# A decoder layer on one core: cross exponentials and the fourth slot's normalisations in other places of ACT's order

## The chip, the cores and the metric

The kernel runs on one core of a Trainium2 chip. The core has a matrix engine (TensorE, PE in the profile, its weight loads PEld), a vector engine (VectorE, DVE), an activation engine (ScalarE, ACT), a general engine (GpSimd, POOL), and SyncE (SP), which issues nearly all transfers here. Each engine takes its own instructions one after another, and semaphores hold an instruction back until what it needs is there. The metric is the device time of one execution in microseconds (us); less is better.

## The reference

One layer of a decoder, in float32, for 32 sequences of 256 tokens with 256 features:

```
x = layernorm(x + self_attention(x))           # 16 query heads, 4 key heads of 64; rotary; alibi bias
x = layernorm(x + cross_attention(x, ctx))     # 16 heads of 16; windows of 64; mask by cell numbers
x = layernorm(x + ffn(x))                      # 256 -> 1024 (gate, up) -> 256, ternary weights, 8 bit rows
```

Self-attention has a softmax over all 256 keys. Cross-attention normalises its query, its context and its output before their projections, rotates queries and keys, and lets a token see the causal part of its own window and the window before it, where the cell numbers agree. The feed-forward rounds its activations by the largest absolute value of a row, and its gate is silu.

## The kernel before

**Periods and slots.** The program is one loop over *slots* (from line 891); four slots, `part` 0 to 3, make a *period* `m`. A sequence has eight self-attention units (128 queries, four heads each), two per period: `2 * m` and `2 * m + 1`. It has four cross-attention units (128 queries, eight heads each), one per period, `k = m - 4`: a sequence's cross-attention runs in the four periods after its self-attention, beside the next sequence's self-attention. So a sequence takes four periods, called P0 to P3 below. Everything else (projections, output projections, normalisations, the feed-forward) is written as generators that yield the number of slots until their next piece; `parts()` runs the pieces that are due in a slot.

**What a unit does.** Self: `self_scores` (L392 on TensorE, name s; then four L408 on DVE, which add the alibi bias and give the negative row maximum nm), `self_exp` (two L426 on ACT per half of the unit; a unit has halves 0 and 1), `self_turn` (eight transposes L453, name t, and two copies L458 on ACT, name pT), `self_values` (L470, name o, and ACT's copy L477, name oT), `self_spread` and `self_normal` (L485, name R; DVE's L493). Cross: `cross_scores` (L662, name xs, and eight L676 on DVE, giving xnm), `cross_exp` (four L692 on ACT per half, name xp), `cross_turn` (L701, name xt, and ACT's copy L703, name xpT), `cross_values` (L717, name xo, and ACT's copy L726, name xoT), `cross_back` (L737, name xr).

**Deferred closures.** Some pieces put a closure on the list `last`, and `flush()` runs the list at the end of the slot (in the kernel before: of every slot). The closures are: in `self_output`, `residual`, with zq (DVE L526) and x1 (ACT L527, then POOL L528); the scalings by ACT of line 197 (`scaled`): the context tokens cs in `cross_inputs`, the cross output on, the two results x of later layernorms; and the store of out. The closures of a fourth slot are, from a period to the next:

- P0 to P1: residual of the sequence's predecessor's second token block (zq, x1);
- P1 to P2: two scalings of cs, which wait for POOL's rstd_zc;
- P2 to P3: the scaling y (L197, the second block's final layernorm of a sequence three places before), its store to out, and residual of the first token block (zq, x1);
- P3 to P0: none.

zq is then transposed on TensorE (name zqT, L203), copied by ACT (zT, L204) and multiplied (xq, L538); ACT adds the bias (L556, name qb). This happens in P1 for one token block and in P3 for the other. In P3, too, fall the gate matmuls of the feed-forward (L804, name ff) and their tanh on ACT (L818), then DVE's L819.

**What sets the order.** For TensorE, DVE and ACT the order is the order in which the program is written (`manual_schedule`, line 888); POOL's and SP's instructions are put in order by the compiler's scheduler. All PSUM tiles come from one pool of eight banks, so an early release by ACT or DVE lets a later matmul begin. The feed-forward's input goes through two transposing transfers on SP (L797, name xiT), and the rotary halves through four transfers (L311, name other, from psin).

Of the kernel before, what the change touches and what calls it, by code (L numbers as in the profile page):

```python
# [50 lines left out]
def kernel(  # L51
# [139 lines left out]
    def flush():  # L191
        while last:
            last.pop(0)()
# [694 lines left out]
    with tc.manual_schedule(engines={mybir.EngineType.PE, mybir.EngineType.DVE, mybir.EngineType.Activation}):  # L888
        running = []
        slot = min(starts)  # L890
        while starts or running:
            m, part = divmod(slot, 4)
            k = m - CROSS
            for gen in starts.pop(slot, ()):
                running.append([slot, gen])

            def cross(f, unit, *more):
                if 0 <= unit < 4 * B:
                    f(*divmod(unit, 4), *more)

            def pair(f, unit):
                if 0 <= unit < 4 * B:
                    f(*divmod(unit, 4))

            def own(f, unit, *more):
                if 0 <= unit < 8 * B:
                    f(*divmod(unit, 8), *more)

            def parts():
                for r in list(running):  # L910
                    if r[0] == slot:
                        wait = next(r[1], r)
                        if wait is r:
                            running.remove(r)
                        else:
                            r[0] += wait or 1

            if part == 0:
                own(self_scores, 2 * m)
                own(self_scores, 2 * m + 1)  # L920
                own(self_exp, 2 * m, 0)
                own(self_exp, 2 * m, 1)
                own(self_exp, 2 * m + 1, 0)
                pair(self_values, m - 1)
                pair(self_spread, m - 1)
                cross(cross_turn, k - 1, 0)
                cross(cross_turn, k - 1, 1)
                own(self_exp, 2 * m + 1, 1)
                parts()
                pair(self_normal, m - 1)  # L930
            elif part == 1:
                parts()
                cross(cross_scores, k)
                cross(cross_values, k - 1)
                cross(cross_exp, k, 0)
            elif part == 2:
                parts()
                cross(cross_exp, k, 1)
                own(self_turn, 2 * m)
                cross(cross_back, k - 1)  # L940
            else:
                pair(self_inverse, m)
                own(self_turn, 2 * m + 1)
                parts()
            flush()
            slot += 1

# [86 lines left out]
```

## Time and profile before

| what | value |
|---|---|
| median of 3 runs | 2207.41 us (2206.43 to 2208.82) |
| the profiled execution's own time | 2208.47 us |
| its span | 2206.7 us |
| granted TensorE clock, mean | 0.984 |
| busy: PE, DVE, ACT, POOL | 96%, 79%, 75%, 50% |
| busy PE from 200 to 2060 us | 1846.04 of 1860 us |

The profile is of one execution. Its span runs from the first to the last instruction of the program; the execution's time lies 1.8 us above it. A group of instructions has its line, engine, operation and `written<-read` names, and how often it came; a wait is named by who waited for whom. The end of a matmul is modelled, so the starts are what to go by. Times in the text are positions in this span unless a unit of difference is meant.

### The profile page before, as it was taken

To read this page: it belongs to the slowest core of one execution; us is meant where nothing else is said; L and a number is where in the kernel's file an instruction comes from. 1 tells how busy PE (TensorE), PEld (TensorE's weight loads), DVE (VectorE), ACT (ScalarE), POOL (GpSimd) and SP (SyncE) were. 2 spreads that over 40 slices of the span, in tenths; PEclk is the share of its full clock that TensorE was granted. 3 is DMA by queue.
4 is the path that set the end of the run, shared out by engine and by line. 5 is a ranking of instruction groups with operands and counts; after the bars stand their busy time and mean duration, and the time that the engine had idled before them with its cause. 6 is when DMAs were issued, how large, how long until landed. Compare 5 with 4: busy or idle time off the path is not lost.

```text
span 2206.7 us, 55094 instructions
## 1 busy us (share of the span) xinstructions
PE 2127.6 (96%) x17766; PEld 1658.8 (75%) x17828; DVE 1742.3 (79%) x6949; ACT 1660.3 (75%) x4961; POOL 1107.7 (50%) x1849
## 2 busy tenths in 40 slices
PE   7899999999999999999999999999999999999984
PEld 5687777777777777777777777777777777777752
DVE  3676888878888878888888888888788887888775
ACT  2578778787778877778877778777778887777862
POOL 4454554555554545554545554545555545555442
PEclk9999999999999999999999999999999999999996
DMA  6322222222222223222222222222222222222111
GB/s 208 94 59 56 68 58 61 60 61 71 70 60 59 64 56 72 70 61 59 64 57 73 68 60 61 61 61 69 71 64 58 61 61 64 71 63 54 31 42 31
DMA packets 191424, 144.05 MB, mean 65 GB/s; under 512 B 107808, under 2 KB 160928, under 8 KB 191136
## 3 DMA queue, kind: packets, MB, share of 16 engines
q1 hardware_dynamic: 189440, 136.95, 25.0%
q8 instruction: 142, 2.33, 0.4%
q10 hardware_dynamic: 1696, 3.57, 0.4%
q14 instruction: 146, 1.20, 0.2%
HBM read 39.50 MB, written 8.39 MB: 22 GB/s over the span
## 4 chain that ended last, share of the span: by engine, by line
PE 77%; ACT 8%; DVE 8%; DMA 2%; issue 2%; POOL 1%; SPq 0%; ACTq 0%; POOLq 0%; DVEq 0%
PE wo L501 10%; PE proj L329 10%; PE t L453 10%; PE s L392 8%; PE o L470 8%; ACT p L426 5%; PE ff L804 4%; PE xt L701 4%; PE xq L538 3%; PE xs L662 3%; PE ffo L851 3%; PE xk L610 3%; PE xv L622 2%; PE R L485 2%; PE xw L763 2%; PE v L361 2%
## 5 line engine op out<-in xcount | busy, mean ns | idle before, releaser
L426 ACT ACTIVATE p<-p,nm 128x256 f32<-128x256 f32 x1024 | 508.3, 499 | 241.8 <-DVE nm L408 241.8
L408 DVE CUSTOM_DVE_ANT_0 p<-s,alibi 128x256 f32<-128x256 f32 x1024 | 361.6, 416 | 3.2 <-PE s L392 3.2
L692 ACT ACTIVATE xp<-xp,xnm 128x128 f32<-128x128 f32 x1024 | 328.5, 401 | 33.8 <-DVE xnm L676 33.8
L458 ACT COPY pT<-t 128x512 f32<-128x512 f32 x512 | 263.9, 598 | 9.4 <-PE t L453 9.2
L453 PE MATMUL t<-ident,p 128*128 128x128 f32 x2048 | 266.0, 273 | 0.9 <-ACT p L426 0.9
L392 PE MATMUL s<-kT,qT 64*128 64x256 f32 x2048 | 259.1, 391 | 0.0
L676 DVE CUSTOM_DVE_ANT_0 xp<-xs,mask 128x128 f32<-128x128 f32 x1024 | 225.7, 286 | 37.2 <-PE xs L662 37.2
L353 POOL TENSOR_TENSOR qT<-qT,other 128x512 f32<-128x512 f32 x128 | 163.2, 1275 | 182.8 <-DMA other<-psin 100.5
L470 PE MATMUL o<-pT,v 128*64 128x256 f32 x2048 | 250.3, 386 | 0.4 <-ACT pT L458 0.4
L329 PE MATMUL proj<-xT,wq_sb 128*128 128x256 f32 x1024 | 245.8, 384 | 0.0
L501 PE MATMUL wo<-wo_sb,oT 128*128 128x256 f32 x1024 | 244.6, 382 | 0.0
L453 PEld LDWEIGHTS t<-ident,p 128*128 128x128 f32 x2048 | 233.7, 141 | 9.2 <-ACT p L426 2.7
L392 PEld LDWEIGHTS s<-kT,qT 64*128 64x128 f32 x2048 | 191.8, 186 | 62.3 <-POOL mask L603 11.9
L501 PEld LDWEIGHTS wo<-wo_sb,oT 128*128 128x128 f32 x1024 | 193.5, 192 | 28.6 <-DVE gu L297 0.3
L470 PEld LDWEIGHTS o<-pT,v 128*64 128x64 f32 x2048 | 136.0, 136 | 99.2 <-issue 31.1
L329 PEld LDWEIGHTS proj<-xT,wq_sb 128*128 128x128 f32 x1024 | 187.7, 193 | 21.6
L426 ACT ACTIVATION_READ_ACCUMULATOR p<-p,nm 128x1 f32 x1024 | 194.0, 189 | 0.0
L493 DVE TENSOR_TENSOR oT<-oT,R 128x512 f32<-128x512 f32 x128 | 87.9, 687 | 104.5 <-ACT oT L477 102.8
L840 POOL TENSOR_SCALAR gu<-gu,ffhup 128x1024 f32<-128x1024 f32 x64 | 72.0, 1125 | 184.5 <-DVE ffhup L836 184.5
L819 DVE SCALAR_TENSOR_TENSOR gu<-gu,ff 128x512 f32<-128x512 f32 x128 | 82.3, 684 | 96.4 <-ACT gu L818 96.4
L600 POOL TENSOR_SCALAR mask<-ck_i,cq_sb 64x128 f32<-64x128 f32 (+1 forms) x96 | 70.3, 732 | 142.7 <-DVE xnm L676 136.7
L703 ACT COPY xpT<-xt 128x512 f32<-128x512 f32 x256 | 135.5, 579 | 0.8 <-PE xt L701 0.7
(148 smaller groups left out, 4480.4 us busy)
## 6 DMA issues: line engine op xcount, KB each, us to landing
other<-psin SPq DMA_DIRECT2D x640, 64.0 KB, 2.0
xT<-in_xt_dram SPq DMA_DIRECT2D x32, 256.0 KB, 2.7
xs<-in_x_dram SPq DMA_DIRECT2D x32, 256.0 KB, 2.7
cs<-in_ctx_dram SPq DMA_DIRECT2D x32, 256.0 KB, 2.8
other<-qb SPq DMA_DIRECT2D x64, 128.0 KB, 2.0
kTz<-tr SPq DMA_DIRECT2D x256, 32.0 KB, 2.0
other<-qb SPq DMA_DIRECT2D x128, 64.0 KB, 1.9
out_dram<-x SPq DMA_DIRECT2D x32, 256.0 KB, 2.1
```

The costliest lines, as they stand in the source:

```text
L329: nc.tensor.matmul(pq[:, c * L : (c + 1) * L], w[:, dc, c * P : (c + 1) * P], xT[:, dc, :], start=(dc == 0), stop=(dc == NDC - 1),)
L353: nc.gpsimd.tensor_tensor(d2, d2, other, ALU.add)
L392: nc.tensor.matmul(banks[half][:, rr * L : (rr + 1) * L], qT[rows_, rr, qc * P : (qc + 1) * P], kT[rows_, kc, :], start=(rr == 0), stop=(r ...
L408: nc.vector.tensor_tensor_reduce(p[:, cols], banks[half][:, cols], alibi[:, 2 * (4 * kc + 2 * rp + rr) + half, :], -0.125, 3.0e38, ALU.add ...
L426: nc.scalar.activation(p[:, cols], p[:, cols], AF.Exp, bias=nm[:, rr : rr + 1], scale=-1.0, accum_out=s["sums", i // 2][:, e : e + 1],)
L453: nc.tensor.transpose(pt[:, j * P : (j + 1) * P], p[half][:, rr * L + kk * P : rr * L + (kk + 1) * P], ident,)
L458: nc.scalar.copy(pT[half], pt)
L470: nc.tensor.matmul(po[half * HD : (half + 1) * HD, rp * L : (rp + 1) * L], s["v"][:, kk, (2 * kc + half) * HD : (2 * kc + half + 1) * HD], ...
L501: nc.tensor.matmul(py[:, 0:D], s["oT", qc, kc][:, r, :], wo_sb[:, 4 * kc + r, :], start=(kc == 0 and r == 0), stop=(kc == 1 and r == 3),)
L676: nc.vector.tensor_tensor_reduce(p[:, cols], banks[2 * half + j // 2][:, j % 2 * P : (j % 2 + 1) * P], s["mask"][:, qc, :], -1.0, 3.0e38, ...
L692: nc.scalar.activation(p[:, cols], p[:, cols], AF.Exp, bias=s["xnm", i][half][:, j : j + 1], scale=-1.0)
L703: nc.scalar.copy(pT, pt)
```

## The change

Three things are put elsewhere in the written order; no instruction is added or removed.

- In the first slot, unit `2 * m`'s exponentials are written straight behind its scores, then the closures of the fourth slot before are run, and then come unit `2 * m + 1`'s scores.
- The fourth slot no longer flushes at its end. Behind the loop a last flush is added for what is left.
- The cross exponentials of half 0 go from the end of the second slot to the third, behind `self_turn(2 * m)`; those of half 1 go from the third slot, ahead of `self_turn(2 * m)`, to the end of the fourth, behind `self_turn(2 * m + 1)` and `parts()`.

```diff
             if part == 0:
                 own(self_scores, 2 * m)
-                own(self_scores, 2 * m + 1)
                 own(self_exp, 2 * m, 0)
                 own(self_exp, 2 * m, 1)
+                flush()
+                own(self_scores, 2 * m + 1)
                 own(self_exp, 2 * m + 1, 0)
                 pair(self_values, m - 1)
                 pair(self_spread, m - 1)
...
                 parts()
                 cross(cross_scores, k)
                 cross(cross_values, k - 1)
-                cross(cross_exp, k, 0)
             elif part == 2:
                 parts()
-                cross(cross_exp, k, 1)
                 own(self_turn, 2 * m)
+                cross(cross_exp, k, 0)
                 cross(cross_back, k - 1)
             else:
                 pair(self_inverse, m)
                 own(self_turn, 2 * m + 1)
                 parts()
-            flush()
+                cross(cross_exp, k, 1)
+            if part < 3:
+                flush()
             slot += 1
+        flush()
```

## The prediction

> **What bounds the kernel now.** I read the page's busy table, then busy time by stage, then the waits, then the order of time at each place where the change moves something.
>
> The page, parts 1 and 2:
>
> ```profile
> PE 2127.6 (96%) x17766; PEld 1658.8 (75%) x17828; DVE 1742.3 (79%) x6949; ACT 1660.3 (75%) x4961; POOL 1107.7 (50%) x1849
> ...
> PE   7899999999999999999999999999999999999984
> ```
>
> Busy time by stage (us; PE, weight loads, DVE, ACT, POOL):
>
> ```profile
> 200.00:2060.00 1860.00, 1846.04 (x15684) 1447.21 (x15738) 1519.46 (x6108) 1464.99 (x4391) 966.11 (x1609) 1.00 0.26 63
> ```
>
> Of these 1860 us TensorE is idle for 14. The waits name nearly all of it (total, times, longest):
>
> ```profile
> ACT p L426 <- DVE nm L408: 241.8, 95, 22.8
> ACT cs L197 <- POOL rstd_zc L185: 87.7, 33, 8.3
> PE xq L538 <- ACT zT L204: 13.5, 32, 0.9
> ```
>
> TensorE runs its written order with one regular pause of about 0.36 us per sequence, before xq; outside it only the first 100 us and the last 150 have idle TensorE time. ACT's long waits cost nothing by themselves. The diff leaves TensorE's order as it is: self_exp, cross_exp and the deferred closures issue nothing there. So the question is where ACT or DVE, in their new order, come late for TensorE.
>
> I call the four periods of a sequence (65.67 us together) P0 to P3; one lies at 1197.83 (P0), 1212.55 (P1), 1227.71 (P2), 1249.66 (P3), 1263.50 (next P0), the times of their first self scores. The pause is in P3. ACT there:
>
> ```profile
> 1247.24 0.63 ACT L197 ACTIVATE x<-x,rstd_y 128x256 f32<-128x256 f32 x1
> 1247.74 0.61 ACT L527 ACTIVATE x<-row,rs_x 128x256 f32<-128x256 f32 x1
> 1252.71 0.51 ACT L426 ACTIVATE p<-p,nm 128x256 f32<-128x256 f32 x1 [4.36 <-DVE nm L408]
> ...
> 1258.09 0.36 ACT L204 COPY zT<-zqT 128x256 f32<-128x256 f32 x1
> ```
>
> TensorE and DVE at the same place:
>
> ```profile
> 1257.49 0.65 PE L717 MATMUL xo<-xpT,xvaug 128*32 128x64 f32 x32
> 1258.50 1.16 PE L538 MATMUL xq<-zT,xq_w 128*128 128x128 f32 x8 [0.36 <-ACT zT L204]
> ```
>
> ```profile
> 1251.37 0.18 DVE L177 BATCH_NORM_AGGREGATE mv_zo<-st 128x2 f32<-128x6 f32 x1
> 1251.46 0.81 DVE L526 TENSOR_SCALAR row<-row,mv_x,rs_x 128x256 f32<-128x256 f32 x1
> 1252.19 0.41 DVE L408 CUSTOM_DVE_ANT_0 p<-s,alibi 128x256 f32<-128x256 f32 x1
> ```
>
> From 1252.71 to zT's end at 1258.45 ACT doesn't pause: whatever is put into this stretch delays xq one for one, and whatever lets it start earlier helps. The first two rows, now ahead of it in 4.36 us of idle time, are what the change puts into it.
>
> **What the Trainium skill says.** Perfetto Trace Analysis, Identifying the Most-Contended Engine: matmul busy time is a bad measure of a tensor bound[...]. I therefore go by starts: eight transposes last 1.04 us in every period, waits or not. The same page, Tensor Engine Instruction: ACT and DVE are strict FIFOs. The trace agrees: at 61.24 ACT has idled 8.29 us at one normalisation while exponentials whose data is ready stand behind it. SBUF — State Buffer, Who interferes with whom: an SBUF tensor_scalar on DVE in a two-port mode and a GpSimd operation exclude each other for a whole instruction; a DVE operation with one SBUF input does not contend. The trace agrees: the L526 row lasts 0.81 us here, under POOL's L574 (until 1252.12), and 0.38 in P1; the L408 rows keep 0.34 us steps under POOL's work.
>
> **The change part by part.** [...]
>
> (a) Flush of the fourth slot, P2 to P3. It holds y (L197), the store of out, zq (DVE L526) and x1 (ACT L527, POOL L528). They go behind the next period's first self unit. On DVE the first L408 no longer stands behind zq: it can start at 1251.46 instead of 1252.19, -0.73 us (its scores, from 1249.66, are ready by about 1250.9). ACT's first exponential then starts at 1251.98. Behind its four, y and x1 take 0.50 us each, start to start (1247.24, 1247.74, and 0.61 less the usual 0.1 overlap): +1.00. The second unit's exponentials don't hide this: their L408 follow zq and have the first half at about 1254.0, and ACT is due there at 1251.98 + 4 x 0.493 + 1.00 = 1254.95. Net +0.27 us at oT's copy, xpT, zT: zT ends at 1258.72, xq starts 0.27 later. On the way xpT's first copy (1256.99) is 0.1 us late for the xs bank that it frees, which the xq wait swallows. y exists from the fourth sequence on: 29 x 0.27 = +7.8. The first three have x1 alone, -0.73 + 0.50 = -0.23; only two wait at xq: -0.3.
>
> (b) The same flush, P0 to P1: zq and x1. L408 starts 0.29 earlier (1213.98 for 1214.27). ACT by (d) is free at 1214.56, not 1214.79: -0.23, then +0.50 for x1: +0.27. zT ends at 1220.80; xq starts at 1220.98 and needs zT 0.04 before, so of 0.41 us cover 0.14 stays: cost nothing, as TensorE's own work hides it. In the last sequence there is no cover (zT 2076.03, xq waits): +0.3.
>
> (c) The same flush, P1 to P2: two context normalisations (cs), which wait for POOL. In the steady sequences the exponentials start earlier and xs, due at 1238.61, has 3 us of cover (xpT's first copy ends at 1235.58): nothing. In the first and last sequence POOL's rstd_zc is late and four ready exponentials (1.97 us) wait behind it:
>
> ```profile
> 62.13 0.60 ACT L197 ACTIVATE cs<-cs,rstd_zc 128x256 f32<-128x256 f32 x1 [0.29 <-POOL rstd_zc L185]
> ```
>
> ```profile
> 67.72 3.78 PE L610 MATMUL xk<-tr,xkv_w 128*128 128x256 f32 x8 [1.59 <-ACT tr L204]
> ...
> 2090.72 0.61 PE L662 MATMUL xs<-kTz,xqT 32*64 32x256 f32 x2 [1.34 <-ACT oT L477]
> ```
>
> They now run before it; tr and oT come 1.97 us earlier, both pauses go: -1.6 and -1.3.
>
> (d) Cross exponentials, from the second and third slot to behind the third's and fourth's pT copies and parts; four last 1.18 us. In P0, pT can start when TensorE's transposes allow (1210.31, as in P2: 0.69 after their first), then two pT (0.96), four exponentials, two pT, four exponentials: 1214.56. In P3 the tanh pair and the pT come before the last four: ACT reaches the next self unit at about 1267.3, before 1267.74. Their readers, the xt transposes, start at 1216.84 and 1267.91: covered by 1.2 us and more (xt's second half). The o matmuls need pT, which come no later. Nothing.
>
> Of the DMAs only the store of out moves. SP's order isn't written by hand: out stands ahead of the turned psin although it is emitted later, so readiness orders the queue. Now y comes after L408, which DVE runs after psin, xvaug and xib, so out should fall behind their eight transfers and block none. POOL's L528 comes about 3 us later (1255.1); should it keep its place, rstd_zo behind it ends by 1257.2, and ACT's normalisation needs it at 1258.6: covered.
>
> After the last self unit (2115 on), the cross exponentials stand behind tanh once (late about 0.5 us for xt), and a pT wait before o (0.42) shrinks: I take +0.1, bounds -1 and +2.
>
> Sum: 7.8 - 0.3 + 0.3 - 1.6 - 1.3 + 0.1 = +5.0 us. The profiled execution took 2208.47 (span 2206.7); the median of the runs is 2207.41, 1.1 lower. Same delta on the median: **2212.4**.
>
> **The rivals.** (1) SP keeps out ahead of psin. Then SP stands until y ends (1254.56); four turned transfers (0.62 each), two of xvaug (0.63), two xiT transposes (1.24) are issued by 1260.8 and the last lands 1.2 later, at 1262.0; gate matmuls are due at 1259.8: 2.3 us x 29 = +66, 2279. For it: out is ahead today; against: its readiness now follows theirs. 0.06.
> (2) P1's cover of 0.14 us doesn't hold: zq or a pT wait costs 0.25 to 0.5 more there; 31 x 0.2 = +6 more, 2218. For it: the smallest cover of all; against: the distance from zT to xq is 0.43 to 0.45 us in nearly every sequence, so little varies. 0.12.
> (3) The seam (a) costs about nothing because y and x1 fall into gaps: only (c) is left, -3: 2204 to 2208, same. Against: ACT has no gap there. 0.10.
> (4) Faster: DVE's earlier start carries further than ACT's 1.00, so that zT also eats into the 0.36 pause. From -0.05 us per sequence on, with (c), the kernel is over 0.2% faster; at the whole pause, 29 x -0.36 - 3 = -13, 2194. For it: the pause is there to be won; against: 0.73 is less than 1.00, and DVE's work before it is unmoved. 0.10.
>
> **How the numbers follow.** Forecast 0.62, spread by 0.1 us per sequence either way: +2 to +8. 0.2% is 4.4 us, about what a measurement of this kernel can tell from no change. Of the forecast 0.36 lies above, 0.26 within. Slower 0.36 + 0.06 + 0.12 = 0.54; same 0.26 + 0.10 = 0.36; faster 0.10. Range 2205 to 2221: it leaves out (1), the far end of (2), and most of (4).
>
> **What would show it.** Right: xq's wait for zT grows from 13.5 to about 21 us; ACT's for rstd_zc nearly goes; L526 stands behind four L408; P3's exponentials start about 0.7 earlier; out follows xiT on SP. Wrong: a new TensorE wait on xs, xt, o or gate in every sequence; a P1 wait for zT; xq's wait unchanged.

## The result, and the profile after

| | before | after |
|---|---|---|
| median of 6 runs each, side by side | 2207.49 us (2205.51 to 2208.82) | 2214.48 us (2211.97 to 2215.04) |
| ratio | | 1.0031, 95% interval 1.0018 to 1.0044 |
| span of the profiled execution | 2206.7 us | 2213.1 us |
| granted clock, mean | 0.984 | 0.986 |

The changed kernel is 0.3% slower: 7.0 us by the medians, 6.4 us by the two spans. The forecast was +5.0.

The page after, parts 1 and 2, and then the busy time by stage (us; PE, weight loads, DVE, ACT, POOL):

```profile
PE 2135.0 (96%) x17828; PEld 1653.6 (75%) x17828; DVE 1709.9 (77%) x6949; ACT 1663.9 (75%) x4961; POOL 1107.7 (50%) x1849
...
PE   7999999999999999999999999999999999999984
```

```profile
200.00:2060.00 1860.00, 1844.84 (x15660) 1438.49 (x15660) 1479.41 (x6073) 1459.20 (x4360) 960.78 (x1601) 1.00 0.26 63
```

TensorE still fills its stretch; 1.2 us less busy time in 1860 is all that this view has to say. (PE's 17828 instructions were 17766 on the page before because 62 records of L804's matmuls are missing there; the weight loads are 17828 in both.) The waits after (total, times, longest) show the signs that the prediction named:

```profile
ACT p L426 <- DVE nm L408: 175.0, 67, 22.7
...
PE xq L538 <- ACT zT L204: 16.8, 34, 0.8
...
ACT cs L197 <- POOL rstd_zc L185: 3.3, 3, 2.8
```

ACT's wait for rstd_zc, 87.7 us before, is down to 3.3. Its waits for nm shrank by 67 us, which by itself bought nothing. xq's wait for zT grew by 3.3 us, less than the 7 or 8 expected. The same P3 as the one that the prediction shows of before, first ACT, then TensorE with xs of before ahead of it, then DVE:

```profile
1253.12 0.51 ACT L426 ACTIVATE p<-p,nm 128x256 f32<-128x256 f32 x1 [2.26 <-DVE nm L408]
...
1255.10 0.59 ACT L197 ACTIVATE x<-x,rstd_y 128x256 f32<-128x256 f32 x1
1255.59 0.59 ACT L527 ACTIVATE x<-row,rs_x 128x256 f32<-128x256 f32 x1
...
1259.48 0.36 ACT L204 COPY zT<-zqT 128x256 f32<-128x256 f32 x1
```

```profile
1256.87 0.69 PE L662 MATMUL xs<-kTz,xqT 32*64 32x256 f32 x16
```

```profile
1258.04 0.80 PE L662 MATMUL xs<-kTz,xqT 32*64 32x256 f32 x16
1258.77 0.65 PE L717 MATMUL xo<-xpT,xvaug 128*32 128x64 f32 x32
1259.89 1.16 PE L538 MATMUL xq<-zT,xq_w 128*128 128x128 f32 x8 [0.47 <-ACT zT L204]
```

```profile
1252.53 0.18 DVE L177 BATCH_NORM_AGGREGATE mv_zo<-st 128x2 f32<-128x6 f32 x1
1252.62 0.39 DVE L408 CUSTOM_DVE_ANT_0 p<-s,alibi 128x256 f32<-128x256 f32 x1
...
1253.97 0.41 DVE L526 TENSOR_SCALAR row<-row,mv_x,rs_x 128x256 f32<-128x256 f32 x1
```

This P3 begins at 1250.82, 1.16 us later than the one of before (1249.66). The first L408 stands at 1252.62, which is 1251.46 + 1.16 to the hundredth; zq follows the four and lasts 0.41 us instead of 0.81; y and x1 stand behind four exponentials; zT ends at 1259.84, 0.23 later than 1258.45 + 1.16 where the prediction had 0.27. xq is late by two pieces. From xs to xo it is 0.73 us instead of 0.62, because the fourth bank of xs waits for xpT's first copy (the 0.1 that the prediction let "the xq wait swallow"); from xo to xq it is 1.12 instead of 1.01. So the wait row grew by half of the cost; the other half is hidden in where xo begins.

**Where the 6.4 us come from.** I cut both spans at two TensorE instructions that each sequence has, its second xq: the fourth sequence's, and that of the last but one. Between them lie 27 sequences. Most have the same length to 0.02 us, which I call the regular length; what the others have above it is the irregular part. There is one such trace of each kernel, so this table is of single executions.

| us | before | after | difference |
|---|---|---|---|
| start, up to the fourth sequence's xq | 300.0 | 295.5 | -4.5 |
| 27 regular sequences | 27 x 65.67 | 27 x 65.80 | +3.5 |
| irregular part of the 27 | 2.9 | 10.2 | +7.3 |
| from the last but one sequence's xq to the end | 130.6 | 130.7 | +0.1 |

A regular sequence costs only half of what was forecast, and the largest term is one that the prediction doesn't have.

**The regular half: something was gained too.** The step from the self scores to o in P0, before and then after:

```profile
1263.50 2.11 PE L392 MATMUL s<-kT,qT 64*128 64x256 f32 x16
1265.53 1.30 PE L470 MATMUL o<-pT,v 128*64 128x256 f32 x10
```

```profile
1264.89 2.00 PE L392 MATMUL s<-kT,qT 64*128 64x256 f32 x16
1266.82 0.87 PE L470 MATMUL o<-pT,v 128*64 128x256 f32 x6
```

2.03 us became 1.93, in every regular sequence (the last counts, x10 and x6, end where the view ends). Before, the score group itself took longer: in the compiled program the banks of its last matmuls were last used by t, and the pT copies freed them late. +0.23 - 0.10 = +0.13, the difference of the regular lengths.

**The irregular part: late transfers.** Ten sequences after are at least 0.6 us over the regular length. In two of them P3's xo alone is late, by 0.6, behind a transfer of qb that took 3.4 us to land. In eight the chain begins at a turned transfer: one of the four of the keys, which POOL adds to kT (L353) about P2's start. What the transfers of 493.5 to 500.5 us were (P2 begins at 500.44), and then those of 427.5 to 434.5, the same stretch of the sequence before it (P2 at 434.63). The columns of the last line are KB each and the median time from issue to landing:

```profile
q8 instruction: 1, 0.02, 0.8%
...
other<-psin SPq DMA_DIRECT2D x4, 64.0 KB, 2.7
```

```profile
q14 instruction: 2, 0.02, 0.8%
...
other<-psin SPq DMA_DIRECT2D x4, 64.0 KB, 2.0
```

What waits for them on POOL and DVE, at 500, and then at 434:

```profile
500.10 1.27 POOL L353 TENSOR_TENSOR kT<-kT,other 128x512 f32<-128x512 f32 x1 [5.01 <-DVE mv_zc L177]
501.35 1.29 POOL L840 TENSOR_SCALAR gu<-gu,ffhup 128x1024 f32<-128x1024 f32 x1
```

```profile
502.68 0.69 DVE L843 TENSOR_SCALAR hib<-gu 128x1024 bf16<-128x1024 f32 x1 [1.02 <-POOL gu L840]
...
504.48 0.41 DVE L408 CUSTOM_DVE_ANT_0 p<-s,alibi 128x256 f32<-128x256 f32 x1
```

```profile
432.96 1.27 POOL L353 TENSOR_TENSOR kT<-kT,other 128x512 f32<-128x512 f32 x1 [3.67 <-DVE ffm L831]
434.21 1.12 POOL L840 TENSOR_SCALAR gu<-gu,ffhup 128x1024 f32<-128x1024 f32 x1
```

```profile
435.60 0.70 DVE L843 TENSOR_SCALAR hib<-gu 128x1024 bf16<-128x1024 f32 x1
...
437.42 0.41 DVE L408 CUSTOM_DVE_ANT_0 p<-s,alibi 128x256 f32<-128x256 f32 x1
```

In the late case the last turned piece lands at 499.94, 1.5 us later against P2's start than at 434; POOL's add of it (L353) begins 1.34 later, POOL's L840 stands behind that add, DVE's L843 waits for L840 with the psin, the qT and all L408 behind it. The first L408 of P2 begins 4.05 us after the scores instead of 2.78. ACT has two scalings of cs to do in the same stretch, and oT's and xpT's copies free the banks of zcT and wo too late:

```profile
509.08 0.93 PE L203 MATMUL zcT<-ident,cs 128*128 128x128 f32 x4
510.05 1.99 PE L501 MATMUL wo<-wo_sb,oT 128*128 128x256 f32 x8
```

```profile
443.28 0.60 PE L203 MATMUL zcT<-ident,cs 128*128 128x128 f32 x4
443.71 1.89 PE L501 MATMUL wo<-wo_sb,oT 128*128 128x256 f32 x8
```

zcT to wo takes 0.97 us instead of 0.43, and wo itself 0.1 more. P3 loses 0.65 besides, at another place. POOL's L573 and DVE's L793 (xib) there, in this sequence and in the regular one shown above:

```profile
523.47 1.26 POOL L573 TENSOR_TENSOR other<-other,rx_sb 128x512 f32<-128x512 f32 x1
523.80 1.22 DVE L793 TENSOR_SCALAR xib<-tr 128x512 bf16<-128x512 f32 x1
```

```profile
1250.60 1.27 POOL L573 TENSOR_TENSOR other<-other,rx_sb 128x512 f32<-128x512 f32 x1
1251.60 0.56 DVE L793 TENSOR_SCALAR xib<-tr 128x512 bf16<-128x512 f32 x1
```

L793 ends 0.28 or 0.29 us after a POOL operation that it overlaps (L572 or L573), in each of the 27 sequences of all eleven traces: DVE stands until POOL is done. Where POOL is late, L793 lasts longer, and L408, ACT and P3's xs with it: 0.66 longer here, and xs loses 0.65. This sequence is 1.29 us longer in all.

Before, a late turned transfer comes in four sequences of 28, after in eight; they have 1.9 us of the irregular part before and 9.1 after. So the number has doubled, and one costs 1.13 us instead of 0.47. By place, P2 from zcT to wo's end lost 0.4 us in the 27 sequences before and 5.2 after, P3 from xs to xq 2.7 and 5.0.

**What makes the transfer late.** The line of queue 8 in the first transfer view is one packet of 16 KB of instructions. There are 142 of them before and 143 after. The Trainium skill (Runtime: NRT & Kernel Launch, Instruction fetch mechanics) says that an engine's instructions are refilled in blocks of 16 KiB, 256 instructions, by a DMA queue of the engine's own, and that the cost of crossing a boundary is mostly hidden. The trace agrees on the size: TensorE, with its weight loads and the waits that are instructions of their own, has 36,441 instructions before (the 62 without a record counted in) and 36,673 after, 257 and 256 per packet, and in both traces fetch number n, counted from 0, begins when TensorE is 152 to 265 instructions past 256 x n. But the traces show a cost that isn't hidden, to transfers of others: I counted, in all eleven traces of this case, the sequences from 200 to 2060 us by whether a fetch on queue 8 begins 1.5 to 3.4 us after the first of the keys' four turned psin transfers is issued.

| | slowest of the four lands over 2.3 us after its issue ends | within 2.3 us |
|---|---|---|
| fetch in that window | 70 | 0 |
| no fetch in it | 4 (a fetch just outside in each) | 234 |

Undisturbed, a piece lands 1.4 us after its issue ends. A sequence has four more such bursts, for the queries; there a fetch in the same window goes with a late piece in 184 cases of 185, but late pieces come without a fetch too (215 of 1056), so other traffic can do it as well. The two qb transfers above also have a fetch, 0.9 and 1.0 us after their issue. So a transfer is late where a fetch falls into it, and how often that happens is a matter of phase: after, 1017 waits stand in TensorE's stream as instructions of their own, before 785 (each with three drains), and a regular sequence has 4.46 fetches instead of 4.43. The change has moved the fetches without touching a matmul. How the two collide inside the DMA engines the traces don't show; nor is it settled why one late transfer costs more after. It lands later there (2.9 to 3.5 us after its issue, before 2.5 to 3.1), but the one at 503.79 before leaves the first L408 as late (4.05 us behind the scores) as the one at 500.44 after, and costs 0.54 us, not 1.29.

### The profile page after: what moved, and what is told of

It is laid out like the page before. It is cut to its first block, busy times and chain, and to the rows that moved or that the text cites. A ratio compares the mean times of both kernels' runs of the same rounds, so it can differ in the third digit from the quotient of the medians.

```text
span 2213.1 us, 55171 instructions
## 1 busy us (share of the span) xinstructions
PE 2135.0 (96%) x17828; PEld 1653.6 (75%) x17828; DVE 1709.9 (77%) x6949; ACT 1663.9 (75%) x4961; POOL 1107.7 (50%) x1849
## 3 DMA queue, kind: packets, MB, share of 16 engines
q10 hardware_dynamic: 1696, 3.57, 0.4%
q14 instruction: 144, 1.18, 0.2%
## 4 chain that ended last, share of the span: by engine, by line
PE 79%; ACT 8%; DVE 5%; POOL 3%; DMA 2%; issue 2%; SPq 0%; POOLq 0%; DVEq 0%; ACTq 0%
PE wo L501 10%; PE t L453 9%; PE s L392 9%; PE o L470 9%; PE proj L329 8%; PE ff L804 5%; ACT p L426 4%; PE xt L701 4%; PE xq L538 3%; PE R L485 3%; PE xs L662 3%; PE xk L610 3%; PE ffo L851 3%; PE xv L622 2%; PE xo L717 2%; PE xw L763 2%
## 5 line engine op out<-in xcount | busy, mean ns | idle before, releaser
L408 DVE CUSTOM_DVE_ANT_0 p<-s,alibi 128x256 f32<-128x256 f32 x1024 | 364.6, 416 | 3.7 <-PE s L392 3.7
L458 ACT COPY pT<-t 128x512 f32<-128x512 f32 x512 | 276.6, 602 | 114.7 <-PE t L453 114.6
L353 POOL TENSOR_TENSOR qT<-qT,other 128x512 f32<-128x512 f32 x128 | 168.6, 1317 | 185.1 <-DMA other<-psin 116.0
L392 PEld LDWEIGHTS s<-kT,qT 64*128 64x128 f32 x2048 | 187.3, 186 | 63.4 <-POOL mask L603 12.3
L701 PE MATMUL xt<-ident,xp 128*128 128x128 f32 x1024 | 135.7, 274 | 1.9 <-ACT xp L692 1.9
```

The costliest lines, as they stand in the source:

```text
L353: nc.gpsimd.tensor_tensor(d2, d2, other, ALU.add)
L392: nc.tensor.matmul(banks[half][:, rr * L : (rr + 1) * L], qT[rows_, rr, qc * P : (qc + 1) * P], kT[rows_, kc, :], start=(rr == 0), stop=(r ...
L408: nc.vector.tensor_tensor_reduce(p[:, cols], banks[half][:, cols], alibi[:, 2 * (4 * kc + 2 * rp + rr) + half, :], -0.125, 3.0e38, ALU.add ...
L458: nc.scalar.copy(pT[half], pt)
L701: nc.tensor.transpose(pt[:, j * P : (j + 1) * P], p[:, j * P : (j + 1) * P], ident)
```

## The experiments

All are timed beside the kernel before on the same chip; the ratio is to it. The last table of this section has all of them cut as above.

**The exponentials alone.** The two `cross_exp` lines as in the change, every flush as before.

> Only the cross exponentials move; every flush stays at the end of its slot, as before. Theory A (the trace after): the 0.107 us that each sequence lost between the last down matmuls, the first self scores and o goes away, because the pT copies stand ahead of four exponentials; nothing else changes: 29 x -0.107 = -3.1 us, about 2204.4, and the step from the s matmuls to o in P0 falls from 2.03 to 1.92 us. xq's wait stays at 13.5 us. Theory B (the prediction's part d): the move is worth nothing, 2207.4, and the gain at o comes from the moved flush.

Measured: 2209.22 us, ratio 1.0013 (1.0007 to 1.0020). The regular sequence has 65.57 us, 0.10 less than before, and the difference lies at o alone: theory A, to the hundredth. The time didn't follow, because six transfers are late instead of four (6.2 us irregular) and the end is 3.3 us longer. The prediction had +0.1 for the end; in this execution TensorE has half clock for 10.2 us from 2133.9, and what part of the 3.3 this is isn't shown.

**The flushes alone.**

> Only the flushes move behind the first self unit; the cross exponentials stay where they were. Theory A: the seam P2 to P3 costs 0.28 us per sequence (29 x 0.28 = +8.2), the first sequences gain 4 to 5, the step to o keeps its 2.03 us: about 2211 without late turned transfers, up to 2216 with as many as the changed kernel has (eight). Theory B (the two halves only work together, the move of the exponentials is what gains in the first sequences): above 2215, with TensorE's wait at xk for zcT's copy back at 1.6 us.

Measured: 2221.30 us, ratio 1.0069 (1.0057 to 1.0081). The start gains 4.6 as expected and the seam costs 0.24 per sequence as expected, but the regular sequence has 66.23 us, 0.56 more than before. TensorE's wait at xk for zcT's copy is gone here, so the first sequences' gain doesn't need the exponentials' move, as theory A has it. The time is over theory A's 2216; it is in the range of theory B, whose reason, the wait at xk, isn't there. The rest of the 0.56 is 0.31 in P0, which neither theory had. TensorE there, of this kernel and of before:

```profile
879.35 1.02 PE L662 MATMUL xs<-kTz,xqT 32*128 32x256 f32 x8
880.30 0.65 PE L717 MATMUL xo<-xpT,xvaug 128*32 128x64 f32 x32
```

```profile
1271.46 0.71 PE L662 MATMUL xs<-kTz,xqT 32*128 32x256 f32 x8
1272.11 0.65 PE L717 MATMUL xo<-xpT,xvaug 128*32 128x64 f32 x32
```

The eight xs take 0.31 us longer: the trace lets the matmul of the fourth bank wait for xpT's first copy. The compiled programs show why. TensorE's order is the same in both, but the allocator hands the eight PSUM banks out otherwise: this xs group's fourth bank was last used by o before, nine groups earlier, and by xt here, seven groups earlier. In the change it is xt's too, but there ACT does the tanh pair 0.6 us sooner after the scores (1.18 us behind them, 1.74 before), as four exponentials have gone behind it, and with it come the L408 and xpT. So the exponentials' move is what pays for the flushes' new banks: -0.10 alone, +0.56 alone, +0.13 together.

**The fetches shifted.**

```diff
+                if j == K_:
+                    for _ in range(32):
+                        nc.tensor.matmul(pb[:, 8:9], ident, ones[:, 0:1], start=True, stop=True)
                 for ch in range(NDC):
```

> The changed kernel with 32 small matmuls of one column added ahead of everything else of its group in the preparation, where TensorE is idle; the results are the same. They shift TensorE's instruction stream by 64 instructions against the work, a quarter of one 16 KB fetch of instructions. Theory A (the fetches are what delays the turned psin in eight sequences): the fetches come 3.8 us earlier against P2, no turned transfer lands late (or one), zcT and wo in P2 wait in none of the sequences, and the time falls by 4 to 5 us to about 2210. Theory B (the lateness in P2 is a regular consequence of the moved work): the same eight sequences or as many, 2214 to 2215.

Each of these matmuls turned out to be four instructions, so the shift was 128, half a fetch, and not 64. Measured: again eight late transfers, but in other sequences: P2 at 439, 572, 704, 837, 1299, 1432, 1564 and 1696 us instead of 368, 500, 633, 766, 1360, 1493, 1626 and 1759. A sequence has 36,673 / 256 / 32, about 4.5, fetches; half a fetch carries each hit into the next sequence. So the lateness belongs to the fetches and not to what these sequences compute. That they can be shifted away, theory A's forecast, failed. The time, 2219.16 us, ratio 1.0060 (1.0045 to 1.0074), says less: the profiled execution, 2215.93 with a span of 2213.1, loses 5.1 us in the start against the change and wins 2.3 at the end, and three of the others took over 2221, for which I have no trace.

**y and x1 behind zT's copy.** Only zq stays in the closure that is flushed behind the first unit; y of the second block, the store of out and x1 get a list of their own, run at the end of the next first slot.

```diff
         def residual():
             nc.vector.tensor_scalar(zq, h, mv[:, 0:1], rs[:, 1:2], ALU.subtract, ALU.mult)
+
+        def kept():
             nc.scalar.activation(x1, h, AF.Identity, bias=rs[:, 2:3], scale=rs[:, 0:1])
...
+            if part == 0:
+                flush_late()
```

> The changed kernel, but of the flush P2 to P3 (and P0 to P1) only zq stays behind the first self unit; y, the store of out and x1 go to the end of the next period's first slot, behind zT's copy. Theory A (y and x1 on ACT ahead of zT are the cost of the seam): zT comes about 1.0 us earlier in P3, the pause before xq and the 0.12 us before xo vanish: 29 x -0.59 = -17, about 2197, xq's wait for zT under 3 us. Theory B (the second unit's first operations on DVE, behind zq, set ACT's pace just as well): zT gains only about 0.3 us, 2206, and ACT shows new pauses before the second unit's exponentials.

Measured: 2187.06 us, ratio 0.9911 (0.9898 to 0.9924), 27 us under the change and 0.9% under the kernel before. TensorE in P3, and its wait over the whole run:

```profile
1244.92 0.65 PE L724 MATMUL xo<-xpT,xvaug 128*32 128x64 f32 x32
1245.50 1.16 PE L545 MATMUL xq<-zT,xq_w 128*128 128x128 f32 x8
```

```profile
PE xq L545 <- ACT zT L208: 3.0, 7, 0.7
```

The pause before xq is gone, and xo isn't late. The regular sequence has 65.13 us, 0.67 less than the change where theory A had 0.59: from xo to xq it is 0.55 less, from xs to xo 0.12. The time is 10 us under theory A's 2197, as the start, the irregular part and the end are shorter too. The fourth bank of this P3's xs is freed by R in this program, and by xt in the kernel before and the change; that needn't have a part, as xs to xo takes 0.62 us with xt's bank in the kernel before as well. P3 has room now: what L793 lasts beyond 0.56 us sums to 4.2 us over the 27 sequences and P3 loses 1.6, in the change 4.8 and 5.0.

**y and x1 back at the fourth slot's end.** The same list, run at its old place:

```diff
-            if part == 0:
+            if part == 3:
                 flush_late()
```

> The changed kernel, but of the flush P2 to P3 (and P0 to P1) only zq on DVE goes behind the first self unit; y, the store of out and x1 are put back to the end of the fourth slot. Theory A (in the sum of the seam, -0.73 from zq on DVE and +1.00 from y and x1 on ACT, each stands by itself): without the +1.00 the regular sequence is as short as with y and x1 behind zT's copy, 65.13 us, and the time is within 3 us of that kernel's 2187. Theory B (y and x1 ahead of the exponentials hold ACT back once its exponentials come 0.7 earlier): between 65.2 and 65.6 us per sequence.

Measured: 2191.56 us, ratio 0.9934 (0.9922 to 0.9946). The regular sequence is 65.13 us again: theory A. It is 4.5 us from the other kernel, not within 3; 3.5 of these are in the irregular part. So the sum of the seam is additive: zq behind the L408 takes 0.44 us off (65.57, the exponentials alone, to 65.13), y and x1 in ACT's unbroken stretch put 0.67 on (65.80). The 0.44 is all of the pause at xq; more than the pause can't be won there.

**One flush alone.** The exponentials moved, and only the flush from P2 to P3 put behind the next first unit (`m % 4 == 2`). This kernel has no last flush: it leaves out the last sequence's second y and its store, so its end says nothing.

> The cross exponentials moved as in the change, and of the flushes only the one from P2 to P3 (y, the store of out, zq, x1) put behind the first self unit; the other two flushes stay at the end of their slots. Theory A (only this flush costs in the regular sequence): 65.57 us (exponentials alone) + 0.23 = 65.80 us per sequence, the same as the whole change; the first sequences gain what the exponentials alone gain there (3.2 us); 2213 to 2216, by how many instruction fetches meet the turned transfer. Theory B (P0 to P1 or P1 to P2 carries part of the cost): under 65.75 us per sequence.

Measured: 65.81 us per regular sequence, theory A; 2212.84 us, just under its 2213, ratio 1.0033 (1.0020 to 1.0045). The flushes from P0 to P1 and from P1 to P2 cost a regular sequence nothing.

**The first context normalisations alone.** Before, with `m == 1`'s flush behind P2's first unit.

> The kernel before, with only the first sequence's context normalisations put behind P2's first self unit. Theory A (the prediction's part c, ready exponentials stand behind a late POOL): TensorE's wait at xk for zcT goes, the first sequences gain 1.6 to 2 us in work, and up to 5 if TensorE is then not stepped down to half clock after the wait; the regular sequence keeps 65.67 us: 2203 to 2206. Theory B (the gain there needs the moved exponentials, or is the clock's own doing): 2207, the fourth sequence's xq at 300 us as before.

Measured: 2203.67 us, ratio 0.9988 (0.9982 to 0.9995): 1.8 us gained, between 1.1 and 4.0, where the prediction's part (c) had 1.6. The profiled execution gains more, 6.4 us in the start; 1.5 of these it has before the change can do anything, at the first scores.

**The other context normalisations back in place.** In both the change and the kernel with y and x1 behind zT's copy:

```diff
-            if part < 3:
+            if part < 3 or (m % 4 == 1 and 1 < m < 4 * B - 3):
                 flush()
```

> The changed kernel, but the context normalisations of all sequences except the first and the last go back to the end of P1's fourth slot. Theory A (behind P2's first unit they lengthen ACT's unbroken stretch, so that a late turned transfer costs more there): the regular sequence keeps 65.80 us, and the time lost in the sequences with a late transfer falls from 1.3 us per late transfer to the 0.4 to 0.8 of the kernel before: 2209 to 2211 in all if again about eight are late. Theory B (only the number of late transfers counts): about 1 us each as before, 2212 to 2215.

> The fastest kernel so far (zq behind the first self unit, y, the store of out and x1 behind zT's copy) with the context normalisations of all sequences but the first and last back at the end of P1's fourth slot. Theory A: 65.13 us per regular sequence, less lost per late turned transfer: 2184 to 2187. Theory B: no difference, 2187 give or take 2 by the number of late transfers.

Measured: 2210.78 us, ratio 1.0028 (1.0020 to 1.0035), and 2186.59 us, ratio 0.9910 (0.9896 to 0.9923). The first has eight late transfers at 8.4 us irregular, 1.05 each, against 1.27 in the change: the cost is near theory B's 1, the time within theory A's range. But its ratio is that of the change (1.0031) within the noise, as the kernel before was faster in these runs, too. The second has seven at 1.0 us, against 4.0 for seven without it, and the same ratio. So single traces point to the scalings of cs as what makes a late transfer dearer, and the times don't show it: not settled.

The executions with a profile, cut as above (us):

| kernel | start | regular | irregular | late of 28 | end | span |
|---|---|---|---|---|---|---|
| before | 300.0 | 65.67 | 2.9 | 4 | 130.6 | 2206.7 |
| the change | 295.5 | 65.80 | 10.2 | 8 | 130.7 | 2213.1 |
| exponentials alone | 296.9 | 65.57 | 6.2 | 6 | 133.9 | 2207.5 |
| flushes alone | 295.4 | 66.23 | 7.5 | 8 | 130.2 | 2221.3 |
| change, fetches shifted | 300.6 | 65.80 | 7.5 | 8 | 128.4 | 2213.1 |
| change, y and x1 behind zT | 294.6 | 65.13 | 4.0 | 7 | 128.2 | 2185.3 |
| change, y and x1 in the old place | 294.7 | 65.13 | 7.5 | 8 | 129.0 | 2189.8 |
| exponentials, and the flush P2 to P3 | 298.8 | 65.81 | 5.5 | 6 | 133.1 | 2214.3 |
| before, first cs behind | 293.7 | 65.67 | 1.4 | 4 | 132.3 | 2200.4 |
| change, cs in place | 295.2 | 65.80 | 8.4 | 8 | 129.0 | 2209.3 |
| y and x1 behind zT, cs in place | 296.3 | 65.13 | 1.0 | 7 | 129.0 | 2184.9 |

## Why the prediction was right in its time, and where it was not

2214.48 lies in the range and 2 us from the forecast; slower was the likeliest sign. But that is in large part luck. 27 regular sequences cost 3.5 us where +0.27 gives 7.3, the start gained 4.5, and the largest term, +7.3, isn't in the sum; without it the pieces of the trace come to -0.9, so the sign hangs on it as well as the number.

- **(a) The seam P2 to P3, +0.27 x 29 = +7.8.** Right, in mechanism and nearly in size: +0.23 us per regular sequence (65.57 to 65.80, and 65.81 with this flush alone), 6.7 for 29. In the trace ACT's first exponential starts 0.75 us earlier against P3's start, and y and x1 take 0.49 each. What the two are worth is shown by undoing the second: 0.44 off and 0.67 on.
- **(b) P0 to P1, nothing.** Right: xq begins 0.17 to 0.18 us after zT's end in nearly every sequence, where 0.14 + 0.04 was worked out. In the last sequence it begins 0.05 after: no cover, as said.
- **(c) P1 to P2.** Nothing in a regular sequence: right. First sequence -1.6: right by the run of this part alone (-1.8). From the first zcT to xk it is 3.86 us instead of 5.82, so tr did come 1.96 earlier; the pause at xk isn't quite gone:

```profile
65.34 0.92 PE L610 MATMUL xk<-tr,xkv_w 128*128 128x256 f32 x3 [0.80 <-ACT tr L204]
```

  The start of the profiled execution fell by 4.5 all the same, and the term was too small for it because the prediction priced work and not the clock. TensorE from 60 to 90 us, before and after (the column behind POOL is the granted clock):

```profile
60.00:90.00 30.00, 25.28 (x134) 19.87 (x134) 16.09 (x41) 16.26 (x51) 13.03 (x17) 0.83 0.33 92
```

```profile
60.00:90.00 30.00, 26.93 (x178) 21.35 (x177) 21.13 (x61) 18.75 (x58) 15.26 (x20) 1.00 0.41 112
```

  Before, half clock was granted for 10.2 us from 63.6, after not at all. The Trainium skill (TensorE: Matmul & The Clock Gate, What's actually happening) has a gate that halves the clock after an idle window of about 3.4 us; the stretches here are 3.4, 6.8 and 10.2 us long and agree with it. The other kernels' profiles have 0 or 3.4 us of it between 60 and 95, those with the old flush at this place too. Whether a wait of 1.59 us at xk or this one execution's luck brought 10.2 stays open, and with it up to 3 us of the -4.5. The kernel with the exponentials alone, which keeps this flush, has its start at 296.9, only 1.4 above the change.
- **(d) The exponentials, nothing.** Wrong by -0.10 x 29 = -2.9. The step that failed is "the o matmuls need pT, which come no later": they come earlier, and the scores before o stand behind them for their banks. I looked at who reads the exponentials, and not at what gains by standing ahead of them.
- **The last sequences, -1.3 + 0.3 + 0.1.** The end is 0.1 longer, where these give -0.9. xs's pause of 1.34 went, as said, and so did the 0.42 before o. But xt waits for xp there three times, 0.67, 0.46 and 0.78 us (at 2139.73, 2150.88 and 2161.16), where the prediction had one wait of 0.5 and the kernel before has none. The scatter of the end between the kernels, 128.2 to 133.9, is larger than this error.
- **What had no term: +7.3** for transfers that meet an instruction fetch, and for DVE standing at L793 behind a POOL that they made late. The prediction read the exclusion of DVE and POOL from L526, and didn't ask where else it held. The trace of before shows the same chain in its sequence at 503.79, where P2's first L408 comes 4.05 us after the scores instead of 2.5; the prediction had not followed a sequence that is longer than the others.
- **SP and POOL.** Right: out follows the xiT transposes (1257.50), and L528 comes later (1256.26) and harms nothing. Rival (1) falls with the first, rival (2) with (b). Rival (3) falls with the run of this one flush. Rival (4) named the right prize, the pause at xq; the change doesn't reach it, and without y and x1 in the way the pause goes entirely.

## What to carry to other kernels

When a closure mixes engines, price each engine's part by itself: here one line on DVE was worth 0.44 us a sequence, the two ACT lines flushed with it cost 0.67, and separating them turned a loss of 0.3% into a gain of 0.9%. Ahead of a tuned, full TensorE, ask of each wait which buffer or bank it is for: moving work that issues nothing on TensorE still gave its groups other banks. And before a difference of some us is laid to the work, count the sequences that are longer than the regular one, look what they have in common, and at which place each of them loses its time.

## What the runs showed of the hardware

- A 16 KB fetch of TensorE's instructions that begins within a burst of four small SBUF transfers made the slowest of them land 2.5 to 3.6 us after its issue instead of 1.4, in 70 cases of 70 for the keys' burst. The sequences with a late one are 0.15 to 1.13 us longer in the mean of a kernel (y and x1 behind zT with cs in place, and the change).
- A wait that the compiler makes an instruction of its own shifts the fetches: 232 more of them on TensorE came with a change that didn't touch TensorE's order.
- The same POOL lock that the prediction read from L526 (0.81 us under POOL's work, 0.38 without) no longer strikes L526 after: behind the L408 it lasts 0.41. At L793 it stays. That ends 0.28 or 0.29 us after POOL's operation in every sequence counted, lasts 0.56 us as a rule and up to 1.43 in the change where POOL is late, and in eight of the change's ten long sequences P3 loses just what it lasts longer, 0.2 to 0.9 us.
